# Seven quarter products for two block products, and projection steps in front of the last two expert outputs

## The chip, the cores and the metric

The kernel runs on one core of a Trainium2 chip, in f32 throughout. The metric is the time of one execution in device microseconds (us). Three executions of the kernel before are shown; their median is the time before.

## The reference, cut to what matters

For each of four sequences of 1024 tokens (1024 channels) the input is normalised, and three projections of it are made. One is scanned along the sequence, one multiplies the scan, the third gates the normalised product, and a fourth projection follows:

```python
q = xn @ Wq;  v = xn @ Wv                    # D = 1024
states = scan(lambda prev, vt: sigmoid(beta) * prev + vt, v)
y = layernorm(q * states) * ln_g + ln_b
attn = (y * silu(xn @ Wg)) @ Wo
```

Beside it stands a mixture of experts on the same normalised tokens: 64 experts, each token goes to the 8 best by softmax, an expert takes up to 128 tokens that are given to it, and its result is added to the token's row with the token's weight:

```python
h = silu(xg @ w1[e].T) * (xg @ v1[e].T)      # 128 tokens, F = 384
out[tok] += wt * (h @ w2[e])
```

The output is x + attn + experts. Tokens at one place of the four sequences share the capacity of an expert in a fixed order, so all routing is known only after the last sequence.

## The kernel before, in words

**Block products.** A projection is a product of 1024 x 1024 weights with 1024 x 1024 activations. It is done by the scheme of Strassen and Winograd: both sides are cut into 2 x 2 blocks of 512, and seven block products replace eight. `left_sums` (L51) makes the sums of weight blocks (slots 4, 5, 3 and 6), `right_sums` (L60) those of the activations (T1 to T4). A *unit* m covers 128 of a block's 512 output channels, so a projection has four units, and each unit has seven block products of four matmuls (128 x 128 weights by 512 columns). `steps` (L138) is a generator that issues them in the order B11, B21, T2, T1, T3, B22, T4 (the names of their right sides): banks `a`, `b` and `c` take the results, ScalarE copies some of them to scratch (`copied`), and VectorE adds. The second product, B21, stands alone in bank `b` and is added to the copy of the first to give c11. `product` (L186) interleaves two units: the last product (T4) of a unit is issued after the first two of the next.

**Rows.** `batch_row` (L596) handles a sequence: v and q of units 0 to 3 in turn (`states`, `queries`), then the gates of units 0 to 3. Routing of the sequence, `take` for the experts' choice, and the next row's preparation are put between. Weights of row 0 are loaded as four blocks and summed on GpSimd; the sums are stored in DRAM (`wsum`), and rows 1 to 3 load them from there, 1792 KB for a unit (`weights`, L577). In rows 1 to 3 all 12 units have the weights of row 0; only the activations differ.

**Preparation of the next row.** `prep(b, h)` (L415) loads 512 tokens of x in two groups of 256, normalises them and stores them in DRAM (`rows`) in an order by quarters. `load_turned(b, h)` (L443) reads them back and turns them on VectorE into the blocks B1h and B2h of the next row. The two groups stay in two buffers of the tag `x` from `prep` to `load_turned`. Half 0 is prepared after q of unit 1 and turned after q of unit 2; half 1 is prepared at the start of the gates and turned before the gate of unit 3, after which the router's logits (`scored`) and the right sums of the next row follow.

**Buffers.** Blocks of activations share nine buffers (`quarter`), weights two (`left`), lines of 1024 six (`line`). PSUM has two banks each for tags a, b, c and one each for t and r; t is used only at the start, for routing tables and by the experts.

**Experts.** `Experts.run` (L1164) goes through the experts in pairs. `hidden` (L978) computes h of one expert by seven products of its own. For pairs, h is turned by one VectorE instruction and 16 ScalarE copies of 32 x 96 (`split_hidden`, `turn_hidden`), issued between the instructions of the next `hidden`; for experts 0 and 1, which stand alone, by three TensorE transposes and one copy (`turn_alone`, L1067). `output` (L1077) multiplies by w2 and scatters to the output with an adding indirect DMA; two scatters go one after the other. Between them stand single steps of the fourth projection (`project`, seven steps for each of 16 units, 112 in all). The list `plan` (L1180) says for each group how many steps stand ahead of the outputs, between and behind. Three steps are left after the last output, and the last block of the fourth projection is joined with a block read back from the output (L1141, L1127), which is stored at the end.

**Order.** In the experts the order on TensorE, VectorE and ScalarE is that of the program (`in_order`). In the rows the framework's planner lays down each engine's order when the kernel is built: it goes by program order among the instructions that its model of time finds ready. `keep_in_program_order` ties an instruction behind the one traced before it on its engine. On the chip each queue is then fixed.

## Time and profile before

| | us |
|---|---|
| median of three runs | 2533.21 (2531.87 to 2533.32) |
| the profiled execution | 2532.91 |
| its span in the profile | 2531.1 |
| TensorE busy | 2518.1 (99%) |
| VectorE busy | 1728.9 (68%) |
| ScalarE busy | 830.0 (33%) |
| GpSimd busy | 757.2 (30%) |
| row 1 and row 2, from the first v to the next row's | about 299 each |
| experts, from the first hidden product | about 1305 |

In a line of the order of time stand the start and the length in us, the engine, the line of the kernel, the operation, the tiles it writes and reads, the shape, how many instructions were merged, and in brackets the idle time of the engine before it with what ended it. PE is TensorE, DVE VectorE, ACT ScalarE, POOL GpSimd, and SPq the queue of loads. Names like `pb_v` tell bank and projection; a row of experts begins with `h`. A record of a matmul is longer than the step to the next one, because matmuls overlap in the array.

### The profile page before, as it was taken

How to read it: one execution, taken by the hardware profiler on the slowest of the kernel's cores; microseconds unless marked ns; L12 is line 12 of the kernel's file. 1: busy time of each engine (PE TensorE's matmuls, PEld its weight loads, DVE VectorE, ACT ScalarE, POOL GpSimd, SP SyncE). 2: the span in 40 equal slices, each digit the busy share in tenths (PEclk: the TensorE clock that was granted, in tenths of full speed). 3: DMA queues.
4: the chain of work that ended last, by engine and by line, in shares of the span. 5: the costliest groups of instructions: out<-in, count | busy, mean ns of one | idle time of the engine just before them, and what ended most of it. 6: DMA issues, size and time to landing. Idle time of an engine off the chain costs nothing. (4 is left out here: it accounts for less than half of the span.)

```text
span 2531.1 us, 23635 instructions
## 1 busy us (share of the span) xinstructions
PE 2518.1 (99%) x8247; PEld 1107.3 (44%) x8247; DVE 1728.9 (68%) x2180; ACT 830.0 (33%) x1960; POOL 757.2 (30%) x629
## 2 busy tenths in 40 slices
PE   9999999999999999999999999999999999999998
PEld 5444444444444444444444444444444444444443
DVE  7857659474684747447786767677676768677674
ACT  3112211131111311022253535444454545444453
POOL 0453301201122110231343434243333435343421
PEclk9999999999999999999999999999999999999999
DMA  5665625543344532145899999999998999999995
GB/s 187 252 201 207 202 81 178 185 143 110 133 154 176 169 142 91 59 172 181 280 339 300 309 315 321 309 299 323 307 330 287 314 314 323 307 299 320 312 322 135
DMA packets 122503, 593.80 MB, mean 235 GB/s; under 512 B 15872, under 2 KB 52736, under 8 KB 89360
## 3 DMA queue, kind: packets, MB, share of 16 engines
q1 hardware_dynamic: 81776, 449.08, 48.3%
q0 software_dynamic: 40176, 143.20, 21.8%
q8 instruction: 65, 1.06, 0.2%
q14 instruction: 54, 0.44, 0.1%
q10 hardware_dynamic: 432, 0.01, 0.0%
HBM read 484.19 MB, written 124.81 MB: 241 GB/s over the span
## 5 line engine op out<-in xcount | busy, mean ns | idle before, releaser
L976 DVE TENSOR_TENSOR t<-w 128x1536 f32<-128x1536 f32 x128 | 224.2, 1752 | 225.6 <-PE hC L995 222.3
L889 POOL DMA_INDIRECT xg<-rows,tables x256 | 285.1, 1114 | 304.4 <-DVE xgT L937 226.2
L1087 POOL DMA_INDIRECT out_dram<-ys,tables x64 | 126.5, 1977 | 387.3 <-issue 134.7
L145 PE MATMUL pa_g<-xT,w 128*128 128x512 f32 x512 | 230.9, 594 | 0.5 <-ACT sc_g L156 0.5
L145 PE MATMUL pa_q<-xT,w 128*128 128x512 f32 x480 | 216.4, 592 | 0.5 <-ACT sc_q L156 0.5
L145 PE MATMUL pa_v<-xT,w 128*128 128x512 f32 x480 | 215.8, 592 | 0.0
L995 PE MATMUL hC<-w,s 128*64 128x384 f32 x512 | 177.3, 489 | 0.0
L995 PE MATMUL hC<-t,s 128*64 128x384 f32 x512 | 177.3, 489 | 0.0
L1083 PE MATMUL hD<-w,act 128*128 128x512 f32 x384 | 175.3, 592 | 0.6 <-ACT act L1072 0.6
L995 PE MATMUL hB<-w,xgT 128*64 128x384 f32 x512 | 175.6, 486 | 0.0
L995 PE MATMUL hA<-w,s 128*64 128x384 f32 x512 | 175.6, 486 | 0.0
L995 PE MATMUL hA<-w,xgT 128*64 128x384 f32 x512 | 175.6, 486 | 0.0
L995 PE MATMUL hD<-t,s 128*64 128x384 f32 x512 | 175.6, 486 | 0.0
L1083 PE MATMUL hT<-w,act 128*128 128x512 f32 x384 | 175.2, 592 | 0.0
L145 PE MATMUL pa_o<-wo_T,gated 128*128 128x512 f32 x384 | 174.3, 596 | 0.0
L145 PEld LDWEIGHTS pa_g<-xT,w 128*128 128x128 f32 x512 | 96.3, 190 | 123.8 <-issue 123.7
L145 PEld LDWEIGHTS pa_q<-xT,w 128*128 128x128 f32 x480 | 91.0, 190 | 115.2 <-issue 113.4
L145 PEld LDWEIGHTS pa_v<-xT,w 128*128 128x128 f32 x480 | 90.9, 190 | 112.9 <-issue 111.7
L719 POOL DMA_DIRECT2D gated<-y x64 | 48.0, 756 | 305.1 <-DVE y L714 290.8
L1061 ACT COPY act<-s 32x96 f32<-32x96 f32 x496 | 133.3, 269 | 7.2
L1061 ACT COPY act<-t 32x96 f32<-32x96 f32 x496 | 133.2, 269 | 6.2
L145 PE MATMUL pc_g<-xT,w 128*128 128x512 f32 x256 | 115.5, 594 | 0.0
(250 smaller groups left out, 4430.7 us busy)
## 6 DMA issues: line engine op xcount, KB each, us to landing
w<-in_w_dram SPq DMA_DIRECT2D x128, 1536.0 KB
w<-in_v_dram SPq DMA_DIRECT2D x64, 1536.0 KB
w<-wsum SPq DMA_DIRECT2D x36, 1792.0 KB
wsum<-w POOLq DMA_DIRECT2D x12, 1792.0 KB
x<-in_x_dram SPq DMA_DIRECT2D x32, 512.0 KB
rows<-x POOLq DMA_DIRECT2D x32, 512.0 KB
gated<-y POOLq DMA_DIRECT2D x64, 256.0 KB
gated<-gated SPq DMA_DIRECT2D x16, 1024.0 KB
```

Source lines behind the costliest of these rows:

```text
L145: nc.tensor.matmul(ps, lhsT=lhs[:, slot, k, :], rhs=blocks[right][:, k, :], start=start and k == 0, stop=stop and k == KH - 1, skip_group_ ...
L719: nc.gpsimd.dma_start(out=gated[b, :, :, slot, m, :].rearrange("u p j -> p u j"), in_=yc[:, h * SH : (h + 1) * SH].rearrange("p (u j) -> p ...
L889: nc.gpsimd.indirect_dma_start(out=self.xg[:, e % 2 * NQ + r, :], out_offset=None, in_=self.rows.rearrange("n (q c) -> (n q) c", q=NQ), in ...
L976: self.nc.vector.tensor_tensor(to, a, b, ALU.subtract)
L995: nc.tensor.matmul(bank[half], lhsT=a[:, ks[k], :], rhs=b[:, ks[k], :], start=(k == 0), stop=(k == len(ks) - 1), tile_position=(0, half.st ...
L1061: self.nc.scalar.copy(self.hT(e)[q * Q : (q + 1) * Q, :, r * Q : (r + 1) * Q], split[r * Q : (r + 1) * Q, :, q, :],)
L1083: nc.tensor.matmul(ps, lhsT=hT[:, j, :], rhs=w2[:, j, cols], start=(j == 0), stop=(j == KF - 1))
L1087: nc.gpsimd.indirect_dma_start(out=self.out, out_offset=bass.IndirectOffsetOnAxis(ap=self.idx[:, e : e + 1], axis=0), in_=ys, in_offset=No ...
```

## The change

In rows 1 to 3 the second block product (B21 on slot 1) of two units, m and m + 1 with m even, is done together: the pair's 256 x 512 left block and the 512 x 512 block B21 are cut once more into 2 x 2, and `inner_steps` issues seven products of two matmuls with 256 columns each. They use two banks of tag b and the bank t. The results go straight to where c11 of both units is collected, so that of unit m + 1 is allocated one unit ahead (`kept`, `ahead`). Odd units issue no second product. The products are issued in three pieces, within the steps of the even unit.

The left sums of the quarters are made on GpSimd in row 0, in the gates of units 0 to 2, for one projection each, and stored in DRAM (`wsum2`). Rows 1 to 3 load them with the weights of even units. The right sums of the quarters are made on VectorE after the outer right sums; T1 of the quarters is written over a part of B21.

The quarters' left and right sums live in one tile, `inside`, which takes one of the two buffers that x had. Preparation and turning therefore work with a single x buffer, one group after the other, and weight w0 of expert 0 goes to the buffer of `inside`.

In the experts, the last pair is turned by `turn_alone`; its two steps of the fourth projection, which stood ahead of both outputs, stand now one in front of each. The diff, cut:

```diff
+NIN = 5
+KQ, SQ = KH // 2, SH // 2
-        return self.three.tile([P, 3, S], F32, tag="x", bufs=2, name=name)
+        return self.three.tile([P, 3, S], F32, tag="x2" if second else "x", bufs=1, name=name)
...
+def inner_steps(nc, pools, lhs, more, blocks, top, bottom, name):
+    lefts = [lhs[:, 1, 0:KQ], lhs[:, 1, KQ:KH]] + [more[:, i] for i in range(NIN)]
+    def acc(ps, slot, right, start=False):
+        for k in range(KQ):
+            nc.tensor.matmul(ps, lhsT=lefts[slot][:, k, :], rhs=blocks[right][:, k, :], ...)
+    def add(to, ps):
+        nc.vector.tensor_tensor(to, to, ps, ALU.add)
+    q0, q1 = slice(0, SQ), slice(SQ, SH)
+    a, c, b = (
+        pools.bank(tag, [P, SH], f"{n}_{name}")[:, q0]
+        for tag, n in (("b", "ia"), ("b", "ic"), ("t", "ib"))
+    )
+    acc(a, 0, "B11", True)
+    nc.scalar.copy(top[:, q0], a)
+    acc(c, 4, "T1", True)
+    nc.scalar.copy(bottom[:, q1], c)
+    acc(b, 1, "B21", True)
+    add(top[:, q0], b)
+    yield
+    acc(a, 5, "T2")
+    nc.scalar.copy(top[:, q1], a)
+    acc(c, 6, "B22")
+    add(top[:, q1], c)
+    acc(a, 3, "T3")
+    add(bottom[:, q1], a)
+    yield
+    acc(a, 2, "T4")
+    nc.scalar.copy(bottom[:, q0], a)
+    yield
...
     s1 = copied(a, 1)
     yield
-    if not begun:
+    if inner is not None:
+        inner = iter(inner)
+        next(inner, None)
+    elif not begun:
         b = pools.bank("b", [P, SH], f"pb_{name}")
         acc(b, 1, "B21", True, True)
     yield
+    if inner is not None:
+        next(inner, None)
+        b = c11
     nc.vector.tensor_tensor(c11, b, s1, ALU.add)
     acc(a, 5, "T2", False, True)
     s2 = copied(a, 2)
     yield
+    if inner is not None:
+        next(inner, None)
     c = pools.bank("c", [P, SH], f"pc_{name}")
...
# prep: each group is loaded, normalised and stored before the next;
# load_turned:
-        for r0, xs, _, _ in stored[b, h]:
+        for g in range(NM // 2):
+            xs = pools.x(f"xq_{b}_{h}_{g}")
             for j in range(2):
...
# sums(b), b > 0:
+            (t,) = inside
+            b21 = quarters[b]["B21"]
+            blocks = {... the four quarters of b21 ...}
+            for _ in right_sums(nc.vector, blocks, lambda n: free.pop()):
+                pass
+            quarters[b]["inner"] = blocks
...
+    def inner_weights(w, pair):
+        load_block(nc, a, wvqg[w], i, o * SH + 2 * pair * P, 2 * P)
+        add = nc.gpsimd.tensor_tensor
+        add(s1, a21, a22, ALU.add)
+        add(s2, s1, a11, ALU.subtract)
+        add(s3, a11, a21, ALU.subtract)
+        add(s4, a12, s2, ALU.subtract)
+        nc.gpsimd.dma_start(out=wsum2[w, pair, :, 0], in_=a22)
+        nc.gpsimd.dma_start(out=wsum2[w, pair, :, 1:], in_=to)
...
             nc.sync.dma_start(out=t, in_=wsum[w, m])
+            if m % 2 == 0:
+                nc.sync.dma_start(out=inner_lefts(), in_=wsum2[w, m // 2])
...
# gates of row 0:
+            if b == 0 and m < NM - 1:
+                for pair in range(NM // 2):
+                    inner_weights(m, pair)
...
# experts:
-        plan += [((e, e + 1), 2, 0, 0) for e in (E - 4, E - 2)]
+        plan += [((E - 4, E - 3), 2, 0, 0), ((E - 2, E - 1), 0, 1, 0)]
-                turning, alone = None, len(group) == 1
+                turning, alone = None, len(group) == 1 or not after
-                    turning = self.turn_hidden(e)
+                    turning = None if alone else self.turn_hidden(e)
-                project(1)
+                project(min(ahead, 1))
...
-                if alone:
-                    self.turn_alone(group[0])
...
-                    if e == group[-1]:
+                    if alone:
+                        self.turn_alone(e)
+                    if alone or i > 0:
                         project(between)
                     self.output(e)
```

More of the change, by code (lines that the diff above doesn't have):

```diff
@@ L123, in __init__, with x @@
         self.ps1 = pool("ps1", 1, PSUM)
-    def x(self, name):
-        return self.three.tile([P, 3, S], F32, tag="x", bufs=2, name=name)
+    def x(self, name, second=False):
+        return self.three.tile([P, 3, S], F32, tag="x2" if second else "x", bufs=1, name=name)
     def y(self, name):
@@ L135, in bank, with steps @@
         return (self.ps1 if tag in "tr" else self.ps2).tile(shape, F32, tag=tag, name=name)
-def steps(nc, pools, lhs, blocks, c11, c12, c22, then, name, begun=None):
+def inner_steps(nc, pools, lhs, more, blocks, top, bottom, name):
+    lefts = [lhs[:, 1, 0:KQ], lhs[:, 1, KQ:KH]] + [more[:, i] for i in range(NIN)]
+    def acc(ps, slot, right, start=False):
+        for k in range(KQ):
+            nc.tensor.matmul(
+                ps,
+                lhsT=lefts[slot][:, k, :],
+                rhs=blocks[right][:, k, :],
+                start=start and k == 0,
+                stop=k == KQ - 1,
+                skip_group_check=True,
+            )
[5 more added lines that the diff above has]
+        for tag, n in (("b", "ia"), ("b", "ic"), ("t", "ib"))
+    )
+    acc(a, 0, "B11", True)
[15 more added lines that the diff above has]
+    yield
+def steps(nc, pools, lhs, blocks, c11, c12, c22, then, name, begun=None, inner=None):
     def acc(ps, slot, right, start, stop):
@@ L183, in steps, with product @@
     then(a)
-def product(nc, pools, lhs, blocks, c11, c12, c22, then, before, name, late=None, begun=None):
-    todo = steps(nc, pools, lhs, blocks, c11, c12, c22, then, name, begun)
+def product(
+    nc, pools, lhs, blocks, c11, c12, c22, then, before, name, late=None, begun=None, inner=None
+):
+    todo = steps(nc, pools, lhs, blocks, c11, c12, c22, then, name, begun, inner)
     next(todo)
@@ L227 @@
     wsum = dram.tile([3, NM, P, NSLOT, KH, P], F32, name="wsum")
+    wsum2 = dram.tile([3, NM // 2, P, NIN, KQ, P], F32, name="wsum2")
     pools = Pools(ctx, tc)
@@ L234 @@
     attn_and_routing(
-        tc, pools, ident, rows, wtab, gated, wsum, x, (wv, wq, wg), beta, ln_g, ln_b, router, out,
+        tc, pools, ident, rows, wtab, gated, wsum, wsum2, x, (wv, wq, wg), beta, ln_g, ln_b, router, out,
         experts.begin, experts.turn_first,
@@ L241, in attn_and_routing @@
 def attn_and_routing(
-    tc, pools, ident, rows, wtab, gated, wsum, x, wvqg, beta, ln_g, ln_b, router, out, routed,
-    turn_first
+    tc, pools, ident, rows, wtab, gated, wsum, wsum2, x, wvqg, beta, ln_g, ln_b, router, out,
+    routed, turn_first
 ):
@@ L319, in prep_first @@
                 blocks[f"B{i + 1}{h + 1}"] = pools.block(f"xT_0_{h}_{i}")
-        groups = [(pools.y if g > 1 else pools.x)(f"x_0_{g}") for g in range(NM)]
+        groups = [pools.y(f"x_0_{g}") if g > 1 else pools.x(f"x_0_{g}", g == 1) for g in range(NM)]
         tiles = [xs[:, j, :] for xs in groups for j in range(2)]
@@ L411, in prep_first @@
         return ws
-    stored = {}
     def prep(b, h):
-        groups = stored[b, h] = []
         for g in range(NM // 2):
@@ L431, in prep @@
             nc.vector.reciprocal(rs, rs)
-            groups.append((r0, xs, mv, rs))
-        for r0, xs, mv, rs in groups:
             for j in range(2):
@@ L448, in load_turned @@
             blocks[f"B{i + 1}{h + 1}"] = pools.block(f"xT_{b}_{h}_{i}")
-        for r0, xs, _, _ in stored[b, h]:
+        for g in range(NM // 2):
+            xs = pools.x(f"xq_{b}_{h}_{g}")
             for j in range(2):
-                from_ = rows[r0 + j * P : r0 + (j + 1) * P, :]
+                n = 2 * g + j
+                r0 = b * S + h * SH + n * P
                 for q in range(NQ):
                     loaded = nc.sync.dma_start(
-                        out=xs[q * Q : (q + 1) * Q, j + 1, :].rearrange("i (r c) -> i r c", r=NQ),
-                        in_=from_[:, q * DQ : (q + 1) * DQ].rearrange("(r i) c -> i r c", i=Q),
+                        out=xs[q * Q : (q + 1) * Q, j, :].rearrange("i (r c) -> i r c", r=NQ),
+                        in_=rows[r0 : r0 + P, q * DQ : (q + 1) * DQ].rearrange(
+                            "(r i) c -> i r c", i=Q
+                        ),
                     )
                     tc.keep_in_program_order(loaded)
-        for g, (_, xs, _, _) in enumerate(stored.pop((b, h))):
-            for j in range(2):
-                n = 2 * g + j
                 for i in range(2):
@@ L465, in load_turned @@
                         ),
-                        xs[:, j + 1, :].rearrange("p (r k j) -> p k r j", r=NQ, j=Q)[
+                        xs[:, j, :].rearrange("p (r k j) -> p k r j", r=NQ, j=Q)[
                             :, i * KH : (i + 1) * KH
@@ L575, in sums, with inner_lefts @@
             pass
+        if b > 0:
+            (t,) = inside
+            b21 = quarters[b]["B21"]
+            blocks = {
+                f"B{i + 1}{j + 1}": b21[:, i * KQ : (i + 1) * KQ, j * SQ : (j + 1) * SQ]
+                for i in range(2)
+                for j in range(2)
+            }
+            free = [
+                t[:, (NIN + 2 * i) * KQ * P : (NIN + 2 * i + 2) * KQ * P].rearrange(
+                    "p (k n) -> p k n", k=KQ
+                )
+                for i in range(3)
+            ]
+            for _ in right_sums(nc.vector, blocks, lambda n: free.pop()):
+                pass
+            quarters[b]["inner"] = blocks
+    inside = []
+    def inner_lefts():
+        (t,) = inside
+        return t[:, 0 : NIN * KQ * P].rearrange("p (s k i) -> p s k i", s=NIN, k=KQ)
+    def inner_weights(w, pair):
+        if not inside:
+            inside.append(pools.x("inside", True).rearrange("p a b -> p (a b)"))
+        (t,) = inside
+        n = KH * 2 * P
+        a = t[:, 0:n].rearrange("p (k n) -> p k n", k=KH)
+        to = t[:, n : 2 * n].rearrange("p (s k i) -> p s k i", s=4, k=KQ)
+        i, o = BLOCKS[1]
+        load_block(nc, a, wvqg[w], i, o * SH + 2 * pair * P, 2 * P)
+        a11, a12, a21, a22 = (
+            a[:, k : k + KQ, c : c + P] for c in (0, P) for k in (0, KQ)
+        )
+        s3, s1, s2, s4 = (to[:, j] for j in range(4))
+        add = nc.gpsimd.tensor_tensor
[5 more added lines that the diff above has]
+        nc.gpsimd.dma_start(out=wsum2[w, pair, :, 1:], in_=to)
     def weights(b, w, m):
@@ L609, in batch_row, with line_of, inner, ahead @@
         waiting = []
+        kept = {}
+        def line_of(name, m):
+            if (name, m) in kept:
+                return kept.pop((name, m))
+            return line.tile([P, S], F32, tag="line", name=f"{name}_{b}_{m}")
+        def inner(m, lhs, top, name, bottom):
+            if b == 0:
+                return None
+            if m % 2 == 1:
+                return ()
+            return inner_steps(
+                nc, pools, lhs, inner_lefts(), quarters[b]["inner"], top, bottom(), f"{name}_{b}_{m}"
+            )
+        def ahead(name, m):
+            t = kept[name, m + 1] = line_of(name, m + 1)
+            return t[:, H0]
         def collect_waiting():
@@ L634, in states @@
         def states(m, left):
-            lo = line.tile([P, S], F32, tag="line", name=f"lo_{b}_{m}")
+            lo = line_of("lo", m)
             hi = line.tile([P, S], F32, tag="line", name=f"hi_{b}_{m}")
@@ L642, in then @@
                 scan(hi[:, H1], hi[:, H1], m + KH, hi[:, SH - 1 : SH])
+            w = weights(b, 0, m)
             left = product(
-                nc, pools, weights(b, 0, m), quarters[b],
+                nc, pools, w, quarters[b],
                 lo[:, H0], lo[:, H1], hi[:, H1], then, left, f"v_{b}_{m}", collect_waiting,
                 begun.get(0) if b == 0 and m == 0 else None,
+                inner(m, w, lo[:, H0], "v", lambda: ahead("lo", m)),
             )
@@ L672, in then @@
                     collect_waiting()
+            w = weights(b, 1, m)
             left = product(
-                nc, pools, weights(b, 1, m), quarters[b],
+                nc, pools, w, quarters[b],
                 y(m, H0), y(m, H1), y(m + KH, H1), then, left, f"q_{b}_{m}", None,
                 begun.get(1) if b == 0 and m == 0 else None,
+                inner(m, w, y(m, H0), "q", lambda: y(m + 1, H0)),
             )
@@ L698, in gates @@
         def gates(m, w, left):
-            lo = line.tile([P, S], F32, tag="line", name=f"glo_{b}_{m}")
+            lo = line_of("glo", m)
             hi = line.tile([P, S], F32, tag="line", name=f"ghi_{b}_{m}")
@@ L726, in gates @@
                 lo[:, H0], lo[:, H1], hi[:, H1], then, left, f"g_{b}_{m}",
-                find_spread if m == 0 else None,
+                find_spread if m == 0 else None, None,
+                inner(m, w, lo[:, H0], "g", lambda: ahead("glo", m)),
             )
@@ L872, in load @@
         if slot not in self.slots:
-            t = (pools.x if e == 0 and n < 2 else pools.y)(f"w{n}_{e}")
+            name = f"w{n}_{e}"
+            t = pools.x(name, n == 0) if e == 0 and n < 2 else pools.y(name)
             self.slots[slot] = t.rearrange("p a b -> p (a b)")
```

## Prediction

> **What bounds the kernel now.** I read the page first, then the waits by engine, then the order of time on TensorE, the queues at the seam between two batch rows, and the last 40 us.

> ```profile
> span 2531.1 us, 23635 instructions
> PE 2518.1 (99%) x8247; PEld 1107.3 (44%) x8247; DVE 1728.9 (68%) x2180; ACT 830.0 (33%) x1960; POOL 757.2 (30%) x629
> PE   9999999999999999999999999999999999999998
> ```

> TensorE is busy in every slice but the last. The list of its waits names six, 4.2 us in all, 2.1 of them at the start. So from 2 to 2522 us time is had only by giving TensorE less to do, and lost by making it wait. The profiled execution took 2532.91 us: its span of 2531.1 and 1.8 around it. The median of the runs shown is 2533.21, 0.3 more; I make the sum against 2532.91 and add the 0.3.

> TensorE in order of time: a block product of row 3, then the 256-column products at the start, and their line by itself.

> ```profile
> 1017.41 3.60 PE L145 MATMUL pa_v<-xT,w 128*128 128x512 f32 x8
> 1020.84 3.60 PE L145 MATMUL pb_v<-xT,w 128*128 128x512 f32 x8
> ...
> 26.74 1.89 PE L355 MATMUL pb<-xT,w 128*128 128x256 f32 x8
> 28.47 1.89 PE L355 MATMUL pa<-xT,w 128*128 128x256 f32 x8
> 30.20 1.89 PE L355 MATMUL pb<-xT,w 128*128 128x256 f32 x8
> ...
> L355 PE MATMUL pa<-xT,w x32: 379/379/483, 12.2 to 30.0; 128*128 128x256 f32 x32
> ```

> Four f32 matmuls leave eight records: each runs as two passes. What a product costs is the step from one start to the next, not the 592 ns of a record, since passes overlap: 1020.84 - 1017.41 = 3.43 us, 0.429 a pass of 512 columns. With 256 columns 30.20 - 28.47 = 1.73 us, 0.2165 a pass, though every pass loads new weights. Half the columns, half the time, with 2 ns on top.

> **The change, part by part.** TensorE waits nowhere in rows 1 to 3 today, so there no part can bring more than the work it takes away.

> *Quarter products (rows 1 to 3).* A pair of units now spends two second products (pb), 2 x 8 x 0.429 = 6.87 us. Instead come seven products of two matmuls of 256 columns, 7 x 2 x 2 x 0.2165 = 6.06. Per pair 0.81 us less, and there are 3 rows x 3 projections x 2 pairs = 18: **-14.5 us**, all on the path. [...] The L355 rows are this very case (128 rows, new weights every pass) and start every 0.2165 us; the row decides.

> *Copies and additions around them.* Each pair adds four ScalarE copies of 256 columns (0.586 us at 512, 0.48 at 384, so by that slope 0.37) and three VectorE additions (0.67 at 512, 0.55 at 384: 0.43). That is 27 us of ScalarE and 23 of VectorE over three rows, which are busy for 51 and 191 of a row's 299 us: beside other work. One hand-over is tight. Bank ia takes product 5, is copied, and takes product 3 on top; only product 6 lies between, 0.87 us. Where the trace shows such a hand-over bare, three transposes, copy, y at 1254.53 to 1255.70, it costs about 0.3 us besides the copies it waits for; 0.3 + 0.37 = 0.67 fits in 0.87 if ScalarE is free. Behind a Silu (1.06) or a table load (1.28) it does not. Bounds: 0 and 1.3 us a pair, 0 to 23 us. ScalarE is busy 17% of a row, and the planner, which lays down each engine's order at build time, can put another product into the hole: I take **+2**. A gain is excluded, since nothing here is on the path today. VectorE's addition out of ia must end before product 2; the outer T2 product, 3.43 us, covers it, and the scans (2.3 and two of 1.2) may stand before it; same treatment, inside the 2.

> *Quarter sums.* Four VectorE operations of 512 columns in each of three rows (0.69): 2.8 us behind the four right sums. T1 is wanted by the second quarter product of v. Today the right sums end at 920.5, and v's first product (920.84) and one quarter product later it is 925.1: 4.6 us for 2.8. Hidden, barely.

> *Loads of quarter sums* (SP, 640 KB, 18 of them). A 1792 KB weight load issued at 704.88 has its last packet at 711.8, 7 us, and is issued 13.7 before its product. 640 KB more is 2.5 us; DMA is busy 36 to 46% in these rows. Hidden. They queue behind the weight load and wait for the quarter products of the pair before; between v and q of one unit pair that is some 14 us ahead of need.

> *Row 0.* GpSimd makes the quarter sums: six loads, 24 additions and 12 stores. An L55 addition takes 1.26 us at 512 columns, so 0.65 at 256, 15.6 us in all, into a queue that stands mostly idle from 245 to 322. The row at 262.39 shows what VectorE pays: two operations of 1.28 take 4.50 while GpSimd adds. [...] Bounds 0 to 6; **+0.5**. SP's loads here wait for the stores of the pair before; the weight loads of g1 to g3 share that queue but have 13.7 us of lead. On GpSimd the additions wait for those loads, and behind them stand the next weights' sums, wanted 10 us into their product.

> *One x buffer in place of two.* This is the dear side of the change. In preparation the second group's loads now wait for the first group's stores to DRAM; in load_turned they wait for the first group's transposes. SP's queue, VectorE's and the last stores on GpSimd are moved past each other. Before:

> ```profile
> 681.26 2.15 SPq L424 DMA_DIRECT2D x<-in_x_dram  x4
> 704.88 0.33 SPq L587 DMA_DIRECT2D w<-wsum  x1
> ...
> 889.07 4.46 PE L145 MATMUL pa_g<-xT,w 128*128 128x512 f32 x10
> 893.36 3.60 PE L145 MATMUL pb_g<-xT,w 128*128 128x512 f32 x8
> ...
> 893.56 2.49 DVE L462 STREAM_TRANSPOSE xT<-x 128x512 f32<-128x512 f32 x4 [1.19 <-PE pa_g L145]
> 897.00 2.49 DVE L462 STREAM_TRANSPOSE xT<-x 128x512 f32<-128x512 f32 x4 [0.94 <-PE pb_g L145]
> ...
> 899.54 7.09 PE L487 MATMUL lg<-xT,r_sb 128*64 128x512 f32 x32
> ```

> Both groups lie loaded by 868, and the transposes wait only for TensorE to leave B11 and B21. Afterwards B21 comes free a product earlier, but half of the first group still waits for B11 (the first product of g3, ending 892.5). Then: two transposes 1.3, eight loads of the second group 1.1 to start and 5.5 to land (2 MB took 857.3 to 867.9), four transposes 2.5: blocks ready near 904.5, logits to 911.5, T1, T2, T4 2.3 each to 918.4, quarter sums T3, T1 to 920. TensorE fills meanwhile with g3's T2, T1, T3, B22 and v's first product (17.2 us) and still has g3's T4 product (3.4) in hand; the quarter T1 is wanted near 921. So it just fits. While VectorE waits for the second group, g3's additions stand behind it, and for these waits g3's T4 product. Bounds per seam: 0, and 10 if the weight load of v (issued within 2 us of the second group's) goes first and nothing fills. I take 0.7 each, **+2**. The preparation at 681 has some 40 us to spare; its danger is the weight load behind it, which the planner may issue first (the experts' load at 898.33 stands ahead of a weight load that was written earlier).

> *Expert weights w0 of expert 0* wait for the x2 buffer until g2's quarter products of row 3, near 1180 instead of 900. DMA moved 181 to 280 GB/s there; 1.5 MB takes 6 us and is wanted by the sum at 1202. Hidden.

> *The last pair.*

> ```profile
> 2494.68 3.70 PE L145 MATMUL pa_o<-wo_T,gated 128*128 128x512 f32 x8
> 2498.22 3.60 PE L145 MATMUL pc_o<-wo_B,gated 128*128 128x512 f32 x8
> 2501.65 2.74 PE L1083 MATMUL hD<-w,act 128*128 128x512 f32 x6
> ...
> 2506.80 2.74 PE L1083 MATMUL hD<-w,act 128*128 128x512 f32 x6
> ...
> 2507.97 1.55 POOL L1087 DMA_INDIRECT out_dram<-ys,tables  x1 [23.68 <-ACT ys L1086]
> 2514.81 1.55 POOL L1087 DMA_INDIRECT out_dram<-ys,tables  x1 [5.29 <-DMA out_dram<-ys,tables]
> ```

> The end hangs on the scatters, one after the other: the second waits for the first to land (6.84 us), then the read of out, the join and the store. Now y of expert 62 ends 12.1 us after 2494.68; with transposes (3 x 0.109) and one step in front it ends at 8.9, its scatter lands at 16.9. y of 63 ends at 17.8 and its scatter goes at 19.0, where it goes at 20.1 today: **-1.0**. TensorE's last step ends at 28.1, before the read lands at 29. The 32 small copies (0.27 each) that leave ScalarE were hidden; the transposes' copies lie under a step.

> **Sum:** 2532.9 - 14.5 - 1.0 + 2 + 0.5 + 2 = 2521.9, with 0.3 to the median **2522**.

> **The rivals.**
> *The hand-overs eat the gain.* For: three banks, seven products of 0.87 us, and a queue with Silu and table loads. Against: the planner has kept TensorE without a gap through such chains. At 0.5 us a pair more: 2522 + 9 = 2531, and the same follows from two bad seams.
> *The seam becomes the bound (slower).* Place: the second group's loads behind the first group's transposes, at three row seams. For: at 893.56 and 897.00 the transposes already wait for TensorE, and now a DMA round follows. Against: 20 us of other products. Price: up to 10 us each, 2522 - 2 + 30 = 2550. It decides above 5 us a seam, and is measurably slower above 7.
> [...]

> **How the numbers follow.** About 0.2% (5 us) can be told from no change: 2528.1 and 2538.3 are the edges. Forecast 0.63 (2517 to 2528); hand-overs 0.19 (2526 to 2537, half of it within the edges); seam 0.15 (three quarters beyond); quarters 0.03. Faster 0.71, same 0.13, slower 0.16. The range 2516 to 2540 leaves out the worst seams and the last rival, 0.15, and a little below.

> **What would show it.** Right: pairs of quarter products 0.87 us apart start to start, rows of about 295 us instead of 299, the scatter of 63 about 19 us after the last hidden product, TensorE's waits under 10 us. Wrong: waits of TensorE for ScalarE copies of ia, for xT transposes or L65 sums at the seam, or 256-column passes above 0.25 us.

## The result, and the profile after

The changed kernel takes **2549.35 us** (median of 4 runs, 2547.9 to 2551.1), the kernel before 2533.24 in the same session. The ratio is 1.0064, 95% interval 1.0051 to 1.0076: slower by 16 us, where 2522 and faster was forecast. The execution that was profiled took 2551.10, 1.8 above that median; its page, the first lines:

```profile
span 2549.0 us, 24281 instructions
PE 2513.8 (99%) x8469; PEld 1150.5 (45%) x8469; DVE 1765.6 (69%) x2244; ACT 848.0 (33%) x2002; POOL 790.6 (31%) x665
PE   9899999999999999999999999999999999999998
```

TensorE has 4 us less of busy time than before (2518.1), in a span that is 18 us longer. The row of tenths shows only one slice lower than before, the second: forty slices of 64 us are too coarse to see stops of 4 us. The list of TensorE's waits (engine, what waited for what: us in total, times, longest) has them:

```profile
PE ia_g L149 <- DVE glo L159: 8.8, 2, 4.7
PE pa_v L193 <- DMA w<-in_wv_dram: 5.7, 1, 5.7
PE ia_v L149 <- ACT lo L174: 3.3, 2, 1.6
PE ia_v L149 <- DVE lo L159: 2.6, 3, 1.5
...
PE pa_v L193 <- POOL w L60: 2.0, 1, 2.0
PE ic_v L149 <- DVE xT L73: 1.1, 2, 0.5
```

None of the six was there before. They add up to 23.5 us; most of the rest is half clock that comes with them (below).

**Where the time went.** For a sum, each TensorE matmul record of both traces was given its steady step (0.429 us with 512 columns, in proportion with fewer, and half of that for the records of 64-column weights, which come in pairs); what passes beyond that until the next record starts is called lost. The steady steps sum to 2494.2 us before and 2479.4 after: 14.8 less. The lost time, by stretch:

| stretch, us from the start | before | after | the last run below |
|---|---|---|---|
| row 0 (45 to 330) | 2.7 | 12.4 | 3.3 |
| row 1 (330 to 628) | 1.2 | 11.9 | 3.5 |
| row 2 (628 to 925) | 1.2 | 11.7 | 3.5 |
| row 3 (925 to 1215) | 1.5 | 4.7 | 3.6 |
| in all, with start and experts | 25.6 | 59.4 | 32.8 |

The span then closes: 2531.1 - 14.8 + 33.8 (59.4 - 25.6), and 1.1 less between the last matmul and the end, is 2549.0. The gain was there in full; 34 us of stops, and of the half clock after them, ate it more than twice.

**The quarter products themselves.** TensorE in order of time, row 1, first gate pair, and then the stop (g0 is the gate of unit 0, v2 the v of unit 2, and so on):

```profile
532.49 1.03 PE L149 MATMUL ia_g<-xT,w 128*128 128x256 f32 x4
533.35 1.03 PE L149 MATMUL ic_g<-xT,inside 128*128 128x256 f32 x4
534.21 1.03 PE L149 MATMUL ib_g<-xT,w 128*128 128x256 f32 x4
535.08 1.03 PE L149 MATMUL ia_g<-inside 128*128 128x256 f32 x4
...
541.10 1.88 PE L193 MATMUL pc_g<-xT,w 128*128 128x512 f32 x4
547.08 2.07 PE L149 MATMUL ia_g<-inside 128*128 128x256 f32 x4 [4.10 <-DVE glo L159]
```

Four passes every 0.86 us: half the columns, half the time, as said. At 547.08 the product waits 4.10 us for a VectorE addition, and then takes 2.07 us where its like takes 1.03. VectorE and SP's queue at the same place:

```profile
536.82 1.22 DVE L788 TENSOR_TENSOR sum<-sum,away 128x1024 f32<-128x1024 f32 x1
542.34 1.93 DVE L352 BATCH_NORM_STATS2 st<-x 128x6 f32<-128x512 f32 x3 [4.30 <-DMA x<-in_x_dram]
...
546.10 0.36 DVE L159 TENSOR_TENSOR glo<-glo,ic_g 128x256 f32<-128x256 f32 x1
...
546.63 0.40 DVE L159 TENSOR_TENSOR glo<-glo,ia_g 128x256 f32<-128x256 f32 x1
...
539.08 0.81 SPq L480 DMA_DIRECT2D x<-in_x_dram  x2
```

Read from the bottom: with one x buffer the load of the second group of the preparation goes out at 539.08, when the first group has been stored. VectorE's next instruction in its queue is the bn_stats (L352) of that group; it stands 4.30 us. Both additions of the quarter products (L159) are queued behind it, their operands long there: TensorE had written ic by 537.0 and ia by 538.7. The stores of the first group went at 532.38 and 534.24 (GpSimd). So a transfer whose tokens are wanted only at the end of the row stops TensorE. Row 2 has the same, 4.66 us at 852.57. At v2 of both rows it is ScalarE: a Sqrt (L486) that waits for the second group's statistics stands ahead of the copy L174 of ia (the third line of the waits).

Row 0, SP's queue, GpSimd and TensorE:

```profile
111.93 8.93 SPq L85 DMA_DIRECT2D inside<-in_wq_dram  x2
120.50 0.37 SPq L85 DMA_DIRECT2D inside<-in_wq_dram  x1
120.98 3.28 SPq L85 DMA_DIRECT2D w<-in_wv_dram  x4
...
119.75 0.72 POOL L674 TENSOR_TENSOR inside<-inside 128x256 f32<-128x256 f32 x1
...
127.16 6.19 PE L193 MATMUL pa_v<-xT,w 128*128 128x512 f32 x7 [5.74 <-DMA w<-in_wv_dram]
```

The code makes the quarter sums of the weights in the gates of row 0. They depend on nothing but a free buffer, and the planner put them some 150 us earlier. The row at 111.93 is two loads. The second goes only at 120.50, when GpSimd has made the last addition of the set before (L674, to 120.47), which still reads the block that the load overwrites; the weights of v2 behind it leave at 120.98 instead of 105.48. The 2.0 us (L60) are the same 40 us earlier: GpSimd's sums for v1 stand behind a quarter sum that waits 9.19 us for its load.

And the windows around the two long stops (busy time of each engine with counts, then granted clock, DMA share, GB/s):

```profile
core 0: us, PE busy (x) PEld busy (x) DVE busy (x) ACT busy (x) POOL busy (x), PEclk, DMA share, GB/s
126.00:133.00 7.00, 5.84 (x7) 2.52 (x8) 0.00 (x0) 0.00 (x0) 4.84 (x7) 0.52 1.09 361
546.00:553.00 7.00, 5.92 (x9) 3.19 (x10) 3.00 (x8) 1.02 (x3) 1.07 (x2) 0.51 0.56 152
```

The granted clock is 0.52 and 0.51 there, and matmuls take twice their time (2.07 us for 1.03 in the rows above): a stop is paid for a second time.

The seam before row 3, where the prediction had seen the way to a slower kernel, went as worked out (VectorE; the pair of the first group that waits for TensorE to leave its block, then the second group):

```profile
917.11 1.30 DVE L517 STREAM_TRANSPOSE xT<-xq 128x512 f32<-128x512 f32 x2 [0.33 <-PE pa_g L193]
923.87 1.30 DVE L517 STREAM_TRANSPOSE xT<-xq 128x512 f32<-128x512 f32 x2 [1.41 <-DMA xq<-rows]
926.23 1.31 DVE L517 STREAM_TRANSPOSE xT<-xq 128x512 f32<-128x512 f32 x2 [1.06 <-DMA xq<-rows]
```

The blocks are ready 10.4 us after the pair at 917.11; 12 had been worked out. TensorE pays only for the quarter sums at the next v: 1.1 us in two seams.

### The profile page after: what moved, and what is told of

Its sections match the earlier page's. It is cut to its first block, busy times and chain, and to the rows that moved or that the text cites. A ratio compares the mean times of both kernels' runs of the same rounds, so it can differ in the third digit from the quotient of the medians.

```text
span 2549.0 us, 24281 instructions
## 1 busy us (share of the span) xinstructions
PE 2513.8 (99%) x8469; PEld 1150.5 (45%) x8469; DVE 1765.6 (69%) x2244; ACT 848.0 (33%) x2002; POOL 790.6 (31%) x665
## 5 line engine op out<-in xcount | busy, mean ns | idle before, releaser
L1022 POOL DMA_INDIRECT xg<-rows,tables x256 | 292.7, 1144 | 292.8 <-DVE xgT L1070 201.7
L1220 POOL DMA_INDIRECT out_dram<-ys,tables x64 | 119.2, 1863 | 390.2 <-issue 162.4
```

What stands on the lines that cost most here:

```text
L1022: nc.gpsimd.indirect_dma_start(out=self.xg[:, e % 2 * NQ + r, :], out_offset=None, in_=self.rows.rearrange("n (q c) -> (n q) c", q=NQ), in ...
L1220: nc.gpsimd.indirect_dma_start(out=self.out, out_offset=bass.IndirectOffsetOnAxis(ap=self.idx[:, e : e + 1], axis=0), in_=ys, in_offset=No ...
```

## The experiments

Twelve kernels were run. Theory A: the stops come from where single instructions stand in the engines' queues, and go when these are moved. Theory B: the new work of row 0 costs wherever it stands. Theory C: the hand-overs of the three banks, or VectorE's load, cost by themselves. Theory D: one x buffer costs by itself.

| run | us | ratio to before, 95% interval |
|---|---|---|
| the changed kernel | 2549.35 | 1.0064 [1.0051, 1.0076] |
| 1 sums held in the gates | 2552.32 | 1.0075 [1.0061, 1.0088] |
| 2 second group one unit later | 2565.32 | 1.0121 [1.0105, 1.0136] |
| 3 before, with one x buffer | 2534.52 | 1.0002 [0.9994, 1.0010] |
| 4 before, with the new last pair | 2532.51 | 0.9995 [0.9987, 1.0003] |
| 5 sums at q2 to q3 | 2565.27 | 1.0121 [1.0106, 1.0137] |
| 6 first group one unit earlier | 2531.75 | 0.9993 [0.9985, 1.0002] |
| 7 both 5 and 6 | 2559.71 | 1.0105 [1.0090, 1.0120] |
| 8 no sums in row 0 | 2539.95 | 1.0024 [1.0015, 1.0033] |
| 9 as 7, row 1's first sum held, first preparation back | 2540.04 | 1.0027 [1.0018, 1.0036] |
| 10 as 6, no sums in row 0 | 2532.67 | 0.9995 [0.9987, 1.0003] |
| 11 as 6, sums from v2 on | 2533.38 | 1.0002 [0.9994, 1.0010] |
| 12 as 11, row 0's first preparation at its old place | 2523.23 | 0.9962 [0.9949, 0.9976] |

**1. Row 0's sums held where they are written.**

```diff
-        load_block(nc, a, wvqg[w], i, o * SH + 2 * pair * P, 2 * P)
+        loaded = nc.sync.dma_start(out=a, in_=...)       # the same block
+        tc.keep_in_program_order(loaded)
```

> The changed kernel, with the loads of row 0's quarter sums (inner_weights) held at the place where they are written, in the gates of row 0, instead of left to the planner, which put them ahead of the weight loads of v1, v2 and q2. Theory A (row 0 loses about 11 us because these loads wait on SP for GpSimd's stores and hold up the weight load of v2, then the clock halves): about 2549 - 11 = 2538; TensorE's waits at 83 and 127 us and the half clock at 126 us are gone. Theory B (GpSimd's additions themselves, or DMA traffic, hold row 0): the wait only moves to the gates of row 0 and the time stays at 2545 to 2550. Theory C (the hand-overs of the three banks cost everywhere): 2549.

Measured 2552.3: A's stops at 83 and 127 us are gone, but B's come, and the time is 2 us above B's range. The waits of TensorE:

```profile
PE var L749 <- DVE sum L824: 4.5, 1, 4.5
PE lg L542 <- DVE xT L517: 3.7, 1, 3.7
...
305.91 7.12 SPq L509 DMA_DIRECT2D xq<-rows  x8
```

The first is at the gates (254 us), where VectorE makes the layer norm's sums while GpSimd adds (1024-column operations of VectorE take 1.53 to 2.28 us there, 1.2 beside an idle GpSimd). The second is the seam: the turned loads of the second group take 7.12 us to issue, 3.65 in the changed kernel. Beside them run GpSimd's last store of the outer weight sums (1792 KB, issued at 306.58; 299.08 in the changed kernel) and stores of `gated`, and the DMA share is 0.99 from 308 to 313; that this traffic is what slows the issue is likely, not shown. Both stops come with 6.83 us of half clock. Row 0 loses 15.6 us here, 12.4 in the changed kernel. So the place that the prediction had assumed for this work costs no less than the place that the planner chose; by the times alone, whose intervals overlap, no more can be said.

**2. The second group of the preparation one unit later.**

```diff
+            if m == 2 and b + 1 < B:
+                prep(b + 1, 0, 1)      # after states(2); group 0 stays after queries(1)
...
+            if m == 0 and b + 1 < B:
+                prep(b + 1, 1, 1)      # after gates(0); first bn_stats held in program order
```

> The changed kernel, with the preparation of the next row cut in two: the second group, which in one x buffer must wait for the first group's stores, is loaded and normalised one unit later, and its first bn_stats is held behind the work written ahead of it. Theory A (VectorE stands in its queue on bn_stats that wait for the second group's late load, with the quarter additions behind; TensorE waits over 4 us at g0 of rows 1 and 2 and then runs at half clock, and 2 to 2.5 us more at v2): about 2549 - 18 = 2531. Theory C (copies and additions of the seven products are late by themselves, whatever stands ahead): no change, 2547 to 2551; the waits of ia's products at g0 stay.

Measured 2565.3: worse, and A's number missed by 34. The bn_stats of the second group no longer wait for their load at g0. But the one held in program order stands behind the layer norm's chain (L840), which waits for the mean; so the Sqrt of their statistics is late on ScalarE, and the copy of ia (L167) behind it, for which TensorE waits:

```profile
548.27 1.23 DVE L840 TENSOR_TENSOR y<-y,y 128x1024 f32<-128x1024 f32 x1 [3.65 <-ACT y L817]
...
553.23 0.29 ACT L488 ACTIVATE rs<-mv,eps 128x2 f32<-128x2 f32 x1 [4.99 <-DVE mv L355]
...
554.46 1.13 PE L149 MATMUL ia_g<-inside 128*128 128x256 f32 x4 [2.39 <-ACT glo L167]
```

In row 0 the late turned loads stopped q2 for 5.7 us. The run doesn't decide between A and C: it removes one late instruction and puts others at the same place.

**3. One x buffer alone** (the preparation and turned loads of the change in the kernel before; no quarter products).

> The kernel before, with one x buffer in place of two alone (preparation and turned loads of the changed kernel, no quarter products). Theory A (the late bn_stats hurt only because quarter products need VectorE within 0.87 us; products of 3.43 us cover the wait): 2533 to 2537. Theory D (one x buffer costs by itself): 2545 to 2555, with TensorE waiting at g0 of rows 1 and 2.

Measured 2534.5 against 2533.8, not to be told from no change: D falls. A's number is right, its reason is not what happened. The bn_stats of the two groups in VectorE's order, row 1:

```profile
503.99 1.26 DVE L293 BATCH_NORM_STATS2 st<-x 128x6 f32<-128x512 f32 x2
...
519.57 1.23 DVE L293 BATCH_NORM_STATS2 st<-x 128x6 f32<-128x512 f32 x2
```

They wait for no load at all. I had supposed that products of 3.43 us cover the wait; what the trace shows is that the planner, with other work around, laid these instructions where the data were there (the second group's load leaves at 513.11; in the changed kernel at 539.08).

**4. The last pair alone** (the two lines of `plan` and what `run` does with them).

> The kernel before, with the last pair of experts alone changed (a step in front of each y). Theory A (the two scatters in a row set the end, and the second goes 1.1 us earlier): 2532.2, 1.0 less than before. Rival (the read of out and the join absorb it): 2533.2, no change.

2532.5 against 2533.8: the size fits, but a microsecond can't be told from nothing by the times. GpSimd's rows show the step itself:

```profile
2504.83 1.55 POOL L1087 DMA_INDIRECT out_dram<-ys,tables  x1 [20.53 <-ACT ys L1086]
2513.74 1.55 POOL L1087 DMA_INDIRECT out_dram<-ys,tables  x1 [7.36 <-ACT ys L1086]
```

The last scatter goes 18.7 us after the last product in front of the pair (2495.08), where it was 20.1; and it waits for y, not for the scatter before it.

**5, 7 and 9. Row 0's sums at q2 to q3,** where GpSimd and DMA stand open; three slots of the buffer in turn, loads held in program order. 5 is this alone, 7 with experiment 6, 9 with one more instruction held.

```diff
+        at, free = turn % 3 * n, (turn + 1) % 3 * n      # a and its sums move on by two slots
...
+            if b == 0 and m == 2:
+                inner_weights(0, 0)                       # after queries(2)
+            if b == 0 and m == NM - 1:                    # after states(3); the last three after queries(3)
+                inner_weights(0, 1); inner_weights(1, 0)
```

> The changed kernel, with row 0's quarter sums at the stretch where GpSimd and the DMA queues stand open (one set behind q2, two around v3, three behind q3, all held in the order of the program), and three slots of the buffer in turn, so that a load no longer waits for the stores of the set before. Theory A (row 0's 11 us come from where the sums stand in SP's, GpSimd's and VectorE's queues, not from the sums themselves): 2549 - 9 to - 11 = 2538 to 2540, no TensorE wait over 1 us in row 0. Theory B (the sums and their traffic cost wherever they stand): 2547 to 2552, with a wait at q3, g0 or the seam of row 0.

> Both moves at once: row 0's quarter sums at q2 to q3, and the first group of each preparation one unit earlier. Theory A (the two causes are separate and add up): 2549 - 25 to - 31 = 2518 to 2524, faster than both kernels. Theory C: 2540 to 2550.

Both missed, by 25 us and by 36 from A's upper end. One row of VectorE in run 7 tells most of it:

```profile
238.20 0.69 DVE L69 TENSOR_TENSOR inside<-xT 128x512 f32<-128x512 f32 x1 [24.72 <-DMA wsum<-inside]
...
239.55 5.38 PE L193 MATMUL pa_q<-xT,w 128*128 128x512 f32 x8 [14.92 <-DVE y L233]
```

L69 is the first quarter sum of row 1's activations. Its operand is ready early, so the planner put it into q3 of row 0; but it writes into the buffer that the weights' sums still use. It waits 24.7 us for their last store, and q3's additions (L233) behind it stop TensorE for 14.9. That is theory A in a place that the move itself had made. Run 9 holds L69 behind g3, and puts row 0's first preparation back to its old place (its Sqrt had stopped q1 for 6.3 us in run 7, see 10):

> The kernel with both moves (quarter sums of row 0 at q2 to q3, first group of each preparation one unit earlier), and two things more: the first quarter sum of row 1 (L69 into the same x2 buffer), which stood in VectorE's queue at q3 of row 0 and waited 24.7 us for the last stores of row 0's sums, is held at the place where it is written, behind g3; and row 0's first preparation stays whole at its old place. Theory A (the 15 us of TensorE at q3 in the two runs with late sums are this one early instruction, not the sums): 2519 to 2525, no TensorE wait over 1 us in row 0. Theory B (GpSimd's sums at q2 to q3 cost by themselves): 2540 to 2560, with the wait at q3 still there.

2540.0, 15 us above A's range and at the very edge of B's. Both stops are gone (19.7 us with their half clock), and two are left at g0:

```profile
PE pa_g L195 <- DMA w<-in_wg_dram: 9.8, 1, 9.8
PE mean L754 <- DVE sum L791: 3.4, 1, 3.4
```

SP issues the weights of g0 from 212.85 on, behind the held loads of the sums; the kernel before issues them from 202.33 on. So B holds for this place, though with the wait at g0 and not at q3: the held loads do catch the next weight load.

**6. The first group of each preparation one unit earlier,** the second where the whole was.

```diff
+            if m == NM - 1 and b + 1 < B:
+                prep(b + 1, 1, 0)      # after states(3); group 1 at the gates as before
...
+                if m == 0:
+                    prep(b + 1, 0, 0)
+                elif m == 1:
+                    prep(b + 1, 0, 1)
```

> The changed kernel, with the first group of each preparation written one unit earlier, so that the second group's load no longer waits for stores of the same moment (the second group stays where the whole was). Theory A (bn_stats that wait for the late load hold up the quarter additions behind them, and TensorE's wait turns into half clock): 2549 - 14 to - 20 = 2529 to 2535; the waits of over 4 us at g0 of rows 1 and 2 and the half clock there are gone. Theory C (VectorE has too much work at g0, whatever the load does, as the run with the second group one unit later may also be read): 2545 to 2560, TensorE still waits for quarter additions or for the sums at g0.

2531.75, inside A's span: 17.6 less than the changed kernel. The lost time of rows 1 and 2 falls from 11.9 and 11.7 to 2.8 and 3.5, with no half clock in them. TensorE's waits, and the bn_stats that stood for 4.3 us:

```profile
PE pa_v L193 <- POOL w L60: 7.0, 1, 7.0
PE ia_v L149 <- DVE lo L159: 3.3, 3, 1.5
...
522.63 1.28 DVE L352 BATCH_NORM_STATS2 st<-x 128x6 f32<-128x512 f32 x2
```

Banks, products, copies and additions are the same as in the changed kernel; so C falls for these 17 us. One stop is left, at v1 of row 0, with half clock behind it.

**8 and 10. No sums in row 0.** Their loads, additions and stores are left out, and rows 1 to 3 load as many bytes of the first left sums, so these two kernels multiply by wrong blocks. 8 is the changed kernel so, 10 is experiment 6 so.

> The changed kernel without row 0's quarter sums: their loads, additions and stores are left out, and rows 1 to 3 load the same number of bytes from the first left sums instead, so the quarter products take wrong left blocks. It bounds what row 0 costs. Theory A (11 us lie in row 0, the rest in rows 1 to 3): 2537 to 2539, with the waits at g0 and v2 of rows 1 and 2 unchanged. Theory C (row 0 is a small part): 2545 to 2549.

> First group of each preparation one unit earlier, and row 0's quarter sums left out (loads, additions, stores; rows 1 to 3 load the same number of bytes from the first left sums, so the quarter products take wrong left blocks). Theory A (the two causes are separate: 2531.75 of the run with the earlier group holds 9 us of row 0): 2521 to 2524. Theory C (something else than these two, such as bare hand-overs of the banks, holds a part): 2527 to 2532.

8: 2539.95, so row 0's sums cost 9.4 as they stood, a little less than A's number (its range is missed by 1 us); g0 and v2 wait as before. 10 missed A (2532.7) and lies just above C's range, but not for C's reason: a Sqrt of ScalarE stops q1 of row 0 for 6.3 us, with half clock:

```profile
118.48 0.29 ACT L486 ACTIVATE rs<-mv,eps 128x2 f32<-128x2 f32 x1 [13.28 <-DVE mv L353]
```

Experiment 6 had moved the first preparation of row 0 into q1, where the choice of tokens fills VectorE; in run 6, where TensorE stops at v1 just before, it does not show.

**11 and 12. The sums from v2 on.** Only the first load is held, behind the first products of v2; the planner places the other five. L69 is held behind g3. 12 puts row 0's first preparation back to its old place.

```diff
+            if b == 0 and m == 2:
+                inner_weights(0, 0)                  # its load held in program order
...
-                if m == 0:
+                if m == (0 if b > 0 else 1):         # 12 only
                     prep(b + 1, 0, 0)
```

> First group of each preparation one unit earlier; of row 0's quarter sums only the first load is held, behind the first products of v2, and the planner places the others after it; the first quarter sum of row 1 is held behind g3. Theory A: no wait at v1 (7.0 us and the half clock after it are gone), 2522 to 2526 if no other weight load is caught behind a load of these sums. Theory B (the loads of the sums, which wait in SP's queue for GpSimd's stores, catch the next weight load wherever they stand): 2528 to 2540, with a TensorE wait at q2, v3 or the gates.

> As the run with both moves and the first load behind v2's first products, and row 0's first preparation whole at its old place, behind q1: one unit earlier it put a Sqrt of ScalarE, which waits for bn_stats on a VectorE that the choice of tokens keeps full there, ahead of the copies of q1 (6.3 us of TensorE and 6.83 us of half clock in that run). Theory A (what is left over the sum of the prediction is only this one stop): 2533.4 - 10 = 2522 to 2525, faster than both kernels by some 9 us. Theory B (row 0's sums cost wherever they stand; a stop goes over to the next place): 2529 to 2536, with a TensorE wait of over 3 us somewhere in row 0.

11: 2533.4. The stop at v1 is gone, and no weight load is caught; its one large wait is the Sqrt of run 10 (119.26, 6.27 us). 12: **2523.2**, ratio 0.9962 (0.9949 to 0.9976), 10 us less than the kernel before and 26 less than the changed one. Its page and its waits:

```profile
span 2522.5 us, 24289 instructions
...
PE ia_v L151 <- DVE lo L161: 3.2, 3, 1.5
...
PE var L753 <- DVE sum L828: 1.2, 1, 1.2
PE ic_v L151 <- DVE xT L75: 1.1, 2, 0.5
```

Same products, same sums, same single x buffer as in the changed kernel: only places in the queues differ. 2531.1 - 14.8 + 7.2 - 1.1 = 2522.4 is its span but for rounding. Row 0 loses 3.3 us with all its sums in it, 0.6 more than in the kernel before, so B falls too.

## Why the prediction was wrong

The changed kernel lies 27 us above the forecast of 2522. Run 12, where the stops of row 0 and of the preparation are gone, lies 1 us above it.

**Quarter products, -14.5: right** (-14.8, in which the last pair's six added transposes stand with +0.7). The row of 256-column products decided it; run 12 has the gain on the clock. No run shows the slower quarters that were given 0.03: in the changed kernel and in run 12 four passes start every 0.86 us, 0.215 a pass, where 0.2165 was taken.

**Copies, additions and seams, +2 and +2, row 0 apart: right in kind, a little low.** Run 12 loses 6.7 us more in rows 1 to 3 than the kernel before (2.3, 2.3 and 2.1), 1.1 of it at the seams, where 2 was forecast, and 3.2 for additions of ia that stand behind other VectorE work.

**The last pair, -1.0: right** (-1.1 between the last matmul and the end).

**Row 0, "+0.5", bounds 0 to 6: wrong, 9.7.** No run shows the 0.5 or its bounds; what they show in its place is VectorE operations of 1.2 us that take 1.53 to 2.28 beside GpSimd's additions (run 1), and a row 0 that loses 0.6 us more than before with all the sums in it (run 12). The failing step is "into a queue that stands mostly idle from 245 to 322". I took the place in the code for the place in the queue. The sums need only a free buffer, and the planner moved them to 71 us. The sentence that weight sums stand behind these loads on GpSimd named the mechanism of the 2.0 us at v1, and gave it no price. SP's queue it named with "13.7 us of lead"; at v2 the weights left 15.5 us later than before. That the assumed place would have been no better (run 1) I did not see either: idle GpSimd isn't idle VectorE or idle DMA.

**"The preparation at 681 has some 40 us to spare; its danger is the weight load behind it": wrong, some 8 us in each of rows 1 and 2.** I asked what stands behind the waiting load in SP's queue. The cost lies with what stands behind the waiting *consumer* in VectorE's (and ScalarE's) queue: additions of the quarter products, wanted within a microsecond. The rows at 536.82 to 546.63 show what I had left out: VectorE stood 4.30 us at the bn_stats and took the two additions behind it only at 546.10 and 546.63, though TensorE had written their operands by 537.0 and 538.7.

**The clock: missing in the sum.** Each of the three stops above 4 us in the changed kernel brought half clock, 17.1 us in all, 15.2 of it after the stops' ends; that is 7.6 us of work. With the waits of 23.5 it makes 31.1 of the 33.8 us.

**The rivals.** "The seam becomes the bound" gave 2550, very near, for a wrong reason: the seam cost 1.1. "The hand-overs eat the gain" named the right bank (ia) with 0.5 us a pair; most of the wait sits there, but in two pairs with 4 to 5 us each, and not for the bank's own sake. The counter "the planner has kept TensorE without a gap through such chains" was the weakest sentence: it speaks of the kernel before, and in the changed one the planner laid a late load's bn_stats ahead of the additions.

What stays open: why the planner put the same bn_stats early with one x buffer alone (run 3) and late with quarter products. Its model of time was not examined.

## What to carry to other kernels

When a buffer is taken away, don't ask only whether the late transfer has slack: find the instruction that consumes it in each engine's queue, and price what is queued behind it. Work without dependencies is the most dangerous to place, since a planner may put it anywhere; hold its first instruction where the trace shows engine *and* DMA open, and look again, since each move made a new first stop. A change whose steps are right can still lose: count the lost time by stretch before giving it up.

## What the runs showed of the hardware that was not expected

The price of a stop is not its length, and whether the clock halves doesn't go by its length alone. Run 2 has two stops of the same kind, of 2.39 us (ending at 554.46) and 2.40 us:

```profile
861.30 2.07 PE L149 MATMUL ia_g<-inside 128*128 128x256 f32 x4 [2.40 <-ACT glo L167]
...
550.48:553.89 3.41, 1.59 (x8) 1.06 (x6) 3.41 (x7) 0.64 (x2) 0.00 (x0) 1.00 0.00 0
553.89:557.30 3.41, 2.84 (x10) 1.82 (x10) 3.41 (x6) 0.80 (x3) 0.57 (x1) 1.00 0.00 0
857.69:861.10 3.41, 1.21 (x6) 0.73 (x4) 3.41 (x7) 1.01 (x3) 0.00 (x0) 1.00 0.00 0
861.10:864.51 3.41, 3.21 (x8) 2.59 (x9) 3.41 (x6) 0.42 (x2) 0.57 (x1) 0.50 0.02 7
```
